# Order of TensorE work in the steps of the two wide cross-attentions: averages first, then transposes, with the turn by features between them

## The chip, the cores and the metric

The kernel runs on one core of a Trainium2 chip. Its time is the device time of one execution in microseconds (us). The core has a matrix engine (TensorE, in the profile PE for its matmuls and PEld for the loads of its stationary operand), a vector engine (VectorE, DVE), a scalar engine (ScalarE, ACT), GpSimd (POOL) and a sync engine (SP) that here only issues DMAs. Matmuls write to PSUM, which has eight banks of 128 x 512 float32; VectorE and ScalarE read it from there. Each engine works through its own list of instructions in order and waits for the others by semaphores.

## The reference

A stack of four layers, each a cross-attention to a context, a mixer and a feed-forward part, works on x of 16 sequences x 64 queries x 256 features. All of it is float32. The change touches the cross-attention of the last two layers, which have the same form (8 heads of 64, context of 16 sequences x 1024 keys x 192 features):

```python
B, Nq, _ = x.shape
q = (x @ Wq).reshape(B, Nq, HEADS, DIM_HEAD)
k = (context @ Wk).reshape(B, context.shape[1], HEADS, DIM_HEAD)
v = (context @ Wv).reshape(B, context.shape[1], HEADS, DIM_HEAD)
sim = jnp.einsum('bihd,bjhd->bhij', q, k) * SCALE
attn = jax.nn.softmax(sim, axis=-1)
out = jnp.einsum('bhij,bjhd->bihd', attn, v)
out = out.reshape(B, Nq, HEADS * DIM_HEAD)
return out @ Wo + bo
```

It is applied as `x = x + attention(_layernorm(x), ctx_768, ...)`. In the layer called L2 a linear recurrence over the 64 queries follows, in L3 a state-space model (Mamba) and then a dense feed-forward.

## The kernel before

`heads64` (lines 420 to 592) computes this attention, once in `L2_xattn_attn` (line 1681) and once in `L3` (line 1840). The keys and values are never formed. The matrix Wk is multiplied into the queries (`queries`, `with_keys`), so that the scores are a product with the raw context, and Wv is multiplied into Wo (`output_matrices`), so that the softmax averages the raw context rows of 192 features.

A tile is 128 rows: two sequences of 64 queries. There are 8 tiles (NT), and each tile has four steps (line 550): a sequence `par` of the two, and a group `g` of four heads. In a step the work on four heads of one sequence is two blocks of 128 rows (2 heads x 64 queries) by 1024 keys. A step's work is spread over three rounds of the loop (line 552). In one round stand

- `now`, the step whose scores are computed: `scores` (line 497) issues 16 matmuls into two PSUM tiles `sc` of two banks each, and `exp_rows` (line 220) then takes each row's maximum on VectorE (`nmx`) and the exponential with its sum on ScalarE (`p`), block 0 first, then block 1;
- `one`, the step of the last round: its two `p` are transposed by `keys_first` (line 228), each in two halves of four 128 x 128 transposes into PSUM tiles `ps_t` (two banks in turn), which are copied out as `pT`: the first half by VectorE and the second by ScalarE, or both by ScalarE where `spare_dve` is set. Then `averages` (line 516) multiplies block 0's `pT` with the context: 8 matmuls of 128 x 192, whose result `o` is divided by the sums into `on`, 192 columns by VectorE (line 522) and 64 of them once more by ScalarE (line 523);
- `two`, the step before that: `averages` of its block 1, and for both blocks `by_features` (line 526), the turn by features: two transposes of `on` into one PSUM tile, copied out in three pieces (`onT`, `onT2`) by `evict` (line 58), which alternates between VectorE and ScalarE, or takes ScalarE alone under `spare_dve`. After a tile's last step `output` multiplies with the output matrices.

`self.misc` hands out the PSUM tile for `averages`, `by_features`, and (in L2) `with_keys`, `queries` and the recurrence. There are two such banks, used strictly in turn, so a new tile waits until the readers of the one before the last are done. In L3 they are called `halves`; there `queries` and `with_keys` take their PSUM (`large`) from the same two banks as `ps_t`.

The order of TensorE's instructions is the order in which the program issues them (`manual_schedule`, line 542). The order on VectorE and ScalarE is set by the scheduler of the framework. `breathe(0)` to `breathe(3)` are places at which another computation puts its next piece: in L2 the recurrence (`go`, line 1801, not at place 3), in L3 the state-space model (`go`, line 2065). The latter first prepares a chunk and then issues items of three VectorE instructions and two exponentials each; while such items are going, `spare_dve` is set. Neither the pieces nor their number per round depend on anything but the count of places passed.

The DMAs of the context are issued by `fetch_cut_ctx` (line 406) ahead of `breathe(0)`, into two buffers in turn.

Of the kernel before, what the change touches and what calls it, by code (L numbers as in the profile page):

```python
# [42 lines left out]
class Net:  # L43
# [376 lines left out]
    def heads64(  # L420
# [12 lines left out]
        def output_matrices():  # L433
            for g in range(2):
                ps = [large([128, 2, D]) for _ in range(2)]
                for v in range(2):
                    hp = 2 * g + v
                    for r in range(2):
                        rows = slice(64 * r, 64 * r + 64)
                        self.mm(ps[r][:, v, :], [(wvT[rows, hp, :128], wo[rows, hp, :])])  # L440
                for r in range(2):
                    to = wvo.rearrange("p (hp r) f -> p r hp f", r=2)[:, r, 2 * g : 2 * g + 2]
                    self.evict(to, ps[r])
            for g in range(2):
                ps = large([128, 2, D])
                for v in range(2):
                    hp = 2 * g + v
                    for r in range(2):
                        rows = slice(64 * r, 64 * r + 64)
                        self.mm(ps[rows, v, :], [(wvT[rows, hp, 128:], wo[rows, hp, :])])  # L450
                self.evict(wvo2[:, 2 * g : 2 * g + 2], ps)

        def normalized(i):

            if i < 2:
                self.carry(i, self.lp.tile([128, 4, D], F32, tag="p", bufs=2, name="p"))
            else:
                self.carry(i, tag="o", bufs=1)
            mv, rs = self.norm_tile(self.xs[:, i, :], 1e-5)
            o = self.lp.tile([128, D], F32, tag="o", bufs=1, name="o")  # L460
            nc.vector.tensor_scalar(o, self.xs[:, i, :], mv[:, 0:1], rs, ALU.subtract, ALU.mult)
            nc.gpsimd.tensor_tensor(self.xs[:, i, :], self.xs[:, i, :], bo, ALU.add)
            hT[i] = self.lp.tile([128, 2, 128], F32, tag="hT", bufs=2, name="hT")
            self.evict(hT[i], self.transposed(o))

        def queries(i):
            ps = large([128, 4, 128])
            for m in range(4):
                self.mm(
                    ps[:, m, :], [(wq[:, c, m * 128 : (m + 1) * 128], hT[i][:, c, :]) for c in range(2)],  # L470
                )
            qT = self.lp.tile([128, 4, 128], F32, tag="qT", bufs=1, name="qT")
            nc.vector.tensor_scalar(qT, ps, 64**-0.5, None, ALU.mult)  # L473

            qpT[i] = qT, [
                [self.lp.tile([128, 8, S], F32, tag=f"qp{n}", bufs=3, name=f"qp{n}") for _ in range(2)]
                for n in range(2)
            ]

        def with_keys(i, n):  # L480

            qT, qp = qpT[i]
            ps = [large([128, 4, 2, S]) for _ in range(2)]
            for hp in range(4):
                for r in range(2):
                    rows = slice(64 * r, 64 * r + 64)
                    self.mm(
                        ps[r][:, hp].rearrange("p b q -> p (b q)"),
                        [(wkT[rows, hp, 128 * n : 128 * n + 128], qT[rows, hp, :])],
                    )  # L490
            for r in range(2):
                for par in range(2):
                    self.evict(
                        qp[n][par].rearrange("p (hp r) q -> p r hp q", r=2)[:, r], ps[r][:, :, par, :]
                    )

        def scores(i, par, g, ctx, between):
            qp = qpT[i][1]
            sc = [self.lps.tile([128, KEYS], F32, tag="sc", bufs=2, name="sc") for _ in range(2)]
            for n in range(2):  # L500
                if n and between is not None:
                    with_keys(*between)
                for u in range(2):
                    h = 4 * g + 2 * u
                    for kh in range(2):
                        rows = slice(64 * kh, 64 * kh + 64) if n else slice(0, 128)
                        at = slice(KEYS, KEYS + 512) if n else bass.ts(kh, 512)
                        nc.tensor.matmul(  # L508
                            sc[u][:, bass.ts(kh, 512)],
                            qp[n][par][rows, h : h + 2, :].rearrange("p h q -> p (h q)"), ctx[0][rows, at],  # L510
                            start=n == 0, stop=n == 1,
                        )
            sums = [self.one_sum() for _ in sc]
            return sums, [self.exp_rows(*x) for x in zip(sc, sums)]

        def averages(pT, sums, ck):
            o = self.misc([128, CD])
            self.mm(o, [(pT[:, t, :], ck[:, t, :]) for t in range(NK)])
            r = self.small.tile([128, 1], F32, name="av_r")
            nc.vector.reciprocal(r, sums)  # L520
            on = self.lp.tile([128, 256], F32, tag="on", bufs=2, name="on")
            nc.vector.tensor_scalar(on[:, :CD], o, r, None, ALU.mult)
            nc.scalar.activation(on[:, CD:], o[:, 128:CD], AF.Copy, scale=r)
            return on

        def by_features(on, onT, par, hp):
            ps = self.transposed(on)
            self.evict(onT[0][:, 2 * hp : 2 * hp + 2, par, :], ps[:, 0, :].rearrange("p (h q) -> p h q", q=S))
            for r in range(2):
                rows = slice(64 * r, 64 * r + 64)  # L530
                self.evict(onT[1][rows, hp, par, :], ps[rows, 1, 64 * r : 64 * r + 64])
# [10 lines left out]
        with self.tc.manual_schedule(engines={mybir.EngineType.PE}):  # L542
            output_matrices()
            first()
            normalized(0)
            queries(0)
            for n in range(2):
                with_keys(0, n)
            normalized(1)
            steps = [(i, par, g) for i in range(NT) for par in range(2) for g in range(2)]  # L550
            one = two = None
            for k in range(len(steps) + 2):
                x = steps[k] if k < len(steps) else None
                now = None
                if x is not None:
                    i, par, g = x
                    if not par and not g:
                        onT = [
                            self.lp.tile([128, 8, 2, S], F32, tag="onT", bufs=1, name="onT"),
                            self.lp.tile([128, 4, 2, S], F32, tag="onT2", bufs=1, name="onT2"),  # L560
                        ]
                    if not g:
                        ctx = self.fetch_cut_ctx(2 * i + par)
                    now = {"x": x, "ctx": ctx, "onT": onT}
                breathe(0)
                if one is not None:
                    one["pT"] = [self.keys_first(one["p"][0])]
                if two is not None:
                    by_features(two["on"], two["onT"], two["x"][1], 2 * two["x"][2])
                    on = averages(two["pT"][1], two["sums"][1], two["ctx"][1])  # L570
                breathe(1)
                if one is not None:
                    one["pT"].append(self.keys_first(one["p"][1]))
                breathe(2)
                if now is not None:
                    between = (i + 1, g) if par and i + 1 < NT else None
                    now["sums"], now["p"] = scores(*x, ctx, between)
                breathe(3)
                if two is not None:
                    by_features(on, two["onT"], two["x"][1], 2 * two["x"][2] + 1)  # L580
                if one is not None:
                    one["on"] = averages(one["pT"][0], one["sums"][0], one["ctx"][1])
                if two is not None and two["x"][1:] == (1, 1):
                    output(two["x"][0], two["onT"])
                    finished(two["x"][0])
                if now is not None and (par, g) == (0, 1):
                    if i + 2 < NT:
                        normalized(i + 2)
                    if i + 1 < NT:
                        queries(i + 1)  # L590
                one, two = now, one
# [1834 lines left out]
```

## Time and profile before

| | us |
|---|---|
| runs shown | 2939.41, 2947.67, 2950.96; median 2947.67 |
| the profiled execution, its own time | 2943.51 |
| its span in the trace | 2941.7 |
| busy: PE, PEld | 2681.1 (91%), 1973.5 |
| busy: DVE, ACT, POOL | 1466.4 (50%), 1043.0 (35%), 306.1 (10%) |
| `heads64` in L2, from its first scores on | 1294 to about 1806 |
| `heads64` in L3, from its first scores on | about 2016 to 2700 |
| mean TensorE clock granted over the span, as a share | 0.952 |

A line of the profile's timeline gives start and duration in us, the engine, the line of the kernel, the operation with its tiles (written <- read), and in brackets the idle time of that engine before it and what ended it. Rows of the same kind that follow each other are merged; such a row's duration reaches from the first start to the last end, and the end of a matmul is modelled, so matmul groups overlap a little. What counts for TensorE is therefore the distance from start to start. A matmul at line 69 is that of the helper `mm`: `ctx,pT` are averages, `w,onT` the output, `hT,w` the queries, `qT,w` the queries with keys. Line 179 with `ident,on` is the turn by features, line 235 a transpose of exponentials, line 508 the scores, line 2054 a sum of the state-space model.

### The profile page before, as it was taken

What the parts mean: (1) busy time and instruction counts of PE and PEld (TensorE: products, weight loads), DVE (VectorE), ACT (ScalarE), POOL (GpSimd) and SP (SyncE); (2) the same over time, 40 slices, a digit from 0 to 9 for tenths busy, and PEclk for the clock granted to TensorE, in tenths of its full rate; (3) what the DMA queues carried; (4) which work ended last, traced back from release to release, by engine and by line L of the source; (5) the groups of instructions that cost most, each with busy time, mean ns of one, the idle gap of its engine ahead of it and who ended that gap; (6) DMA issues with size and microseconds to landing.
All of it is one profiled execution on the core that took longest, in us unless ns stands there. A gap on an engine that the chain in (4) does not pass through costs nothing. (4 is left out here: it accounts for less than half of the span.)

```text
span 2941.7 us, 42834 instructions
## 1 busy us (share of the span) xinstructions
PE 2681.1 (91%) x16972; PEld 1973.5 (67%) x16972; DVE 1466.4 (50%) x3120; ACT 1043.0 (35%) x2350; POOL 306.1 (10%) x407
## 2 busy tenths in 40 slices
PE   7887898999999898989999998898998898888999
PEld 3556785566666586867777776795766666666777
DVE  2555113666666653234444444323446656658593
ACT  1322121555555441223333322122334455455330
POOL 1111232100000011310101001101001000000000
PEclk9897998999999997989999999899999999999999
DMA  8512772111010113811111111552213213121110
GB/s 235 167 49 81 279 270 73 35 30 36 27 37 23 41 37 137 298 53 45 56 56 45 44 54 61 214 218 75 69 43 87 70 42 94 54 73 29 57 45 8
DMA packets 79221, 253.57 MB, mean 86 GB/s; under 512 B 15151, under 2 KB 26954, under 8 KB 69290
## 3 DMA queue, kind: packets, MB, share of 16 engines
q1 hardware_dynamic: 59562, 165.01, 18.1%
q0 software_dynamic: 13312, 80.28, 8.0%
q10 hardware_dynamic: 6144, 5.51, 0.5%
q8 instruction: 135, 2.21, 0.3%
q14 instruction: 68, 0.56, 0.1%
HBM read 233.80 MB, written 14.82 MB: 85 GB/s over the span
## 5 line engine op out<-in xcount | busy, mean ns | idle before, releaser
L223 DVE TENSOR_REDUCE nmx<-sc 128x1 f32<-128x1024 f32 x264 | 311.9, 1219 | 223.8 <-PE sc L508 132.8
L225 ACT ACTIVATE p<-sc,nmx 128x1024 f32<-128x1024 f32 x264 | 294.6, 1116 | 312.8 <-DVE nmx L223 312.2
L508 PE MATMUL sc<-ctxT,qp 128*128 128x512 f32 (+1 forms) x1024 | 357.0, 603 | 0.0
L508 PEld LDWEIGHTS sc<-ctxT,qp 128*128 128x128 f32 (+1 forms) x1024 | 139.5, 190 | 154.8 <-issue 152.6
L69 PE MATMUL halves<-ctx,pT 128*128 128x192 f32 x1024 | 188.0, 339 | 9.4 <-DVE xs L89 4.0
L69 PEld LDWEIGHTS halves<-ctx,pT 128*128 128x128 f32 x1024 | 175.7, 200 | 12.3 <-DVE xs L89 4.5
L69 PE MATMUL misc<-ctx,pT 128*128 128x192 f32 x1024 | 177.6, 327 | 0.5 <-DVE qT L473 0.5
L235 PE MATMUL ps_t<-ident,p 128*128 128x128 f32 x1088 | 147.6, 278 | 25.2 <-ACT p L225 17.6
L69 PEld LDWEIGHTS misc<-ctx,pT 128*128 128x128 f32 x1024 | 166.3, 191 | 2.2 <-DVE qT L473 1.0
L2020 ACT ACTIVATE da<-rep,al 128x252 f32<-128x252 f32 x256 | 115.1, 498 | 117.8 <-DVE x L2030 101.1
L2030 DVE TENSOR_TENSOR_SCAN x<-da,x 128x512 f32<-128x512 f32 x128 | 152.9, 1220 | 3.4 <-ACT da L2020 2.8
L237 ACT COPY pT<-ps_t 128x512 f32<-128x512 f32 x182 | 104.3, 585 | 140.3 <-PE ps_t L235 138.4
L235 PEld LDWEIGHTS ps_t<-ident,p 128*128 128x128 f32 x1088 | 127.4, 143 | 39.2 <-ACT p L225 22.4
L235 PE MATMUL misc<-ident,p 128*128 128x128 f32 x1024 | 138.3, 280 | 13.4 <-ACT p L225 6.3
L235 PEld LDWEIGHTS misc<-ident,p 128*128 128x128 f32 x1024 | 110.7, 141 | 39.7 <-ACT p L225 14.4
L160 POOL TENSOR_TENSOR ln_rs<-ln_ve,nhalf 128x1 f32<-128x1 f32 x80 | 45.7, 576 | 691.7 <-DVE ln_ve L158 552.7
L237 ACT COPY pT<-misc 128x512 f32<-128x512 f32 x128 | 75.0, 586 | 115.4 <-PE misc L235 115.0
L69 PE MATMUL ps_h<-r,w 128*128 128x256 f32 x512 | 113.4, 381 | 0.0
L69 PE MATMUL gu<-dT,wa 128*128 128x128 f32 (+1 forms) x864 | 104.8, 280 | 3.9 <-ACT dT L64 2.4
L239 DVE COPY pT<-misc 128x512 f32<-128x512 f32 x128 | 88.3, 690 | 38.8 <-PE misc L235 28.2
L69 PEld LDWEIGHTS ps_h<-r,w 128*128 128x128 f32 x512 | 96.6, 190 | 15.9 <-issue 2.5
L69 PEld LDWEIGHTS gu<-dT,wa 128*128 128x128 f32 (+1 forms) x864 | 98.3, 185 | 11.2 <-ACT dT L64 4.8
(478 smaller groups left out, 4479.1 us busy)
## 6 DMA issues: line engine op xcount, KB each, us to landing
ctx<-in_ctx SPq DMA_DIRECT2D x48, 768.0 KB
ctxT<-in_ctxT SPq DMA_DIRECT2D x48, 512.0 KB
w<-in_L2f_W SPq DMA_DIRECT2D x24, 1024.0 KB
rep<-dus SPq DMA_DIRECT2D x256, 64.0 KB
ctxT<-in_ctxT SPq DMA_DIRECT2D x16, 768.0 KB
ctxT<-in_ctxT SPq DMA_DIRECT2D x96, 128.0 KB
ys<-yb ACTq DMA_DIRECT2D x40, 128.0 KB
bc_rep<-bcs SPq DMA_DIRECT2D x32, 128.0 KB
```

The costliest lines, as they stand in the source:

```text
L69: self.nc.tensor.matmul(out, lhsT, rhs, start=n == 0, stop=n == len(pairs) - 1)
L160: nc.gpsimd.tensor_tensor(rs, ve, self.nhalf, ALU.pow)
L223: self.nc.vector.tensor_reduce(nmx, sc, AX.X, ALU.max, negate=True)
L225: self.nc.scalar.activation(p, sc, AF.Exp, bias=nmx, accum_out=sums)
L235: self.nc.tensor.transpose(ps[:, u, :], p[:, at : at + 128], self.ident)
L237: self.nc.scalar.copy(pT[:, 4 * g : 4 * g + 4, :], ps)
L239: self.nc.vector.tensor_copy(pT[:, 0:4, :], ps)
L508: nc.tensor.matmul(sc[u][:, bass.ts(kh, 512)], qp[n][par][rows, h : h + 2, :].rearrange("p h q -> p (h q)"), ctx[0][rows, at], start=n == ...
L2020: nc.scalar.activation(da[:, g, :, 1:], now[j][:, 0, :].rearrange("p (b s) -> p b s", s=S)[:, :, 1:], AF.Exp, scale=al[:, col : col + 1],)
L2030: nc.vector.tensor_tensor_scan(flat, da.rearrange("p g b s -> p (g b s)"), flat, 0.0, ALU.mult, ALU.add)
```

## The change

In each round, `averages` of the step before last (block 1) moves from behind the first transposes to the very start, ahead of them. The turn by features of that step's block 0, which stood between those transposes and the averages, now follows behind `breathe(1)`, ahead of the second transposes. So the order of a round's first half goes from

first transposes, turn by features, averages, `breathe(1)`, second transposes

to

averages, first transposes, `breathe(1)`, turn by features, second transposes.

The second half of the round (scores, the turn by features of block 1, averages of the last step's block 0, output, the next tile's queries) stays as it was. No instruction is added or taken away.

```diff
                 breathe(0)
+
+
+                if two is not None:
+                    on = averages(two["pT"][1], two["sums"][1], two["ctx"][1])
                 if one is not None:
                     one["pT"] = [self.keys_first(one["p"][0])]
+                breathe(1)
                 if two is not None:
                     by_features(two["on"], two["onT"], two["x"][1], 2 * two["x"][2])
-                    on = averages(two["pT"][1], two["sums"][1], two["ctx"][1])
-                breathe(1)
                 if one is not None:
                     one["pT"].append(self.keys_first(one["p"][1]))
                 breathe(2)
```

## The prediction

> **What bounds the kernel now.** I read the page's busy times first, then the longest waits of TensorE, then the timeline of single rounds in each of the two stages, and last the table of busy time and granted clock by stretches.
>
> ```profile
> PE 2681.1 (91%) x16972; PEld 1973.5 (67%) x16972; DVE 1466.4 (50%) x3120; ACT 1043.0 (35%) x2350; POOL 306.1 (10%) x407
> ```
>
> TensorE is busy 91% of the span and no work leaves it, so only its waits can move the time. The two attentions differ in these. In L2 (1294 to 1806) the timeline of TensorE shows waits of 0.3 us or more only some two or three times in the 63 us of a tile. An ordinary round there, with VectorE and ScalarE beside it:
>
> ```profile
> 1344.69 2.77 PE L69 MATMUL misc<-ctx,pT 128*128 128x192 f32 x16
> ...
> 1346.12 1.11 ACT L225 ACTIVATE p<-sc,nmx 128x1024 f32<-128x1024 f32 x1
> ...
> 1347.23 0.19 ACT L64 COPY onT<-misc 64x64 f32<-64x64 f32 x1
> 1347.29 1.04 PE L235 MATMUL ps_t<-ident,p 128*128 128x128 f32 x8
> ...
> 1347.55 0.23 DVE L62 COPY onT<-misc 64x64 f32<-64x64 f32 x1
> ...
> 1348.38 0.65 PE L179 MATMUL misc<-ident,on 128*128 128x128 f32 x2
> ```
>
> The first transposes (1347.29) follow the averages (1344.69) after 2.60 without a wait: their exponentials are long done. But the copies of the turn by features that preceded those averages end only at 1347.78, since one stands on ScalarE behind the second exponential, and the last waits for it.
>
> In L3 the state-space model fills VectorE and ScalarE from about 2250 on, and there TensorE waits for the exponential:
>
> ```profile
> 2317.20 2.77 PE L69 MATMUL halves<-ctx,pT 128*128 128x192 f32 x16
> ...
> 2319.07 2.35 DVE L223 TENSOR_REDUCE nmx<-sc 128x1 f32<-128x1024 f32 x2
> 2320.32 1.11 ACT L225 ACTIVATE p<-sc,nmx 128x1024 f32<-128x1024 f32 x1 [1.42 <-DVE nmx L223]
> ...
> 2321.43 0.57 ACT L64 COPY onT<-halves 128x128 f32<-128x128 f32 x3
> ...
> 2321.58 1.09 PE L235 MATMUL ps_t<-ident,p 128*128 128x128 f32 x8 [1.61 <-ACT p L225]
> ...
> 2323.89 0.58 PE L179 MATMUL halves<-ident,on 128*128 128x128 f32 x2 [1.22 <-DVE on L522]
> ```
>
> The maximum (2319.07) comes late because VectorE works off items first; two waits follow, 1.61 and 1.22. There are five such rounds (first transposes at 2279, 2300, 2321, 2488, 2509).
>
> **The change, part by part.** Call X the averages at a round's end, Y those that move to the next round's start. Nothing is added; one order changes. DMAs don't move: they are issued ahead of place 0. Y frees its context buffer 1 to 3 us earlier, which only helps the load that waits for it on SP.
>
> *1. A new wait ahead of Y.* The PSUM bank of Y is that of the turn by features before X. Y could start at 1347.29 and must wait for the copy ending at 1347.78. Where `output` waits for such a copy, it starts 0.05 later (copy to 1374.55, matmul at 1374.60), and averages that waited last 2.87, not 2.77. So 0.49 + 0.05 + 0.10 = 0.64 here. The same subtraction in the 23 such rounds of L2 and the 6 of L3 ahead of the state-space model gives 0.5 to 1.4, mean 0.72: 29 x 0.72 = **+20.9**.
>
> *2. A wait that goes.* The turn by features follows its `on` by one group of transposes today: 1348.38 - 1347.29 = 1.09, where 0.88 is the distance without waiting (2192.99 to 2193.87), and 0.48 on to the next averages, where it is 0.22 (2193.87 to 2194.09). That is 0.47; where the copies fall the other way (1424.55) 0.24. With Y in between it is covered: 29 x -0.36 = **-10.4**. What is late next is part 3.
>
> *3. Transposes closer together.* Both `ps_t` banks are filled by the first transposes, and the second ones need them empty. Today Y (2.6) lies between. Without work at place 1 only the turn does: second transposes 0.88 + 0.22 = 1.10 after the first. The first copy ends 1.33 after its transposes start (1351.46 to 1352.79), with 0.05 for the handover 1.38: 0.28 late, 0.05 more for a start after a wait. ScalarE's copy ends 1.66 after, when 1.82 is needed, so it adds nothing. In 32 rounds (the 29 and three tile ends with place 1 empty): **+10.6**. Bounds: 0 if VectorE's copy gains 0.3, double if `on` of Y, ahead of it on VectorE, is held up. Queued behind these copies are only the maxima of the next scores, which end 5.5 later.
>
> So the regular rounds lose 20.9 - 10.4 + 10.6 = **+21**.
>
> *4. Queries in L3.* They share the banks of `ps_t`; the second half of the first transposes waits for their eviction: 0.35, 0.35, 0.99, 1.96, 2.89, 0.40 = 6.9. Y (2.6) now lies between, 6.6 could go. In the rounds of 1.96 and 2.89 VectorE is working off items, and part returns at its next result: **-5**, between 0 and -6.6.
>
> *5. Place 1.* Pieces there wait for `on` of Y to leave its bank: 0.74, 1.38 in L2, 2.16, 3.27, 1.50, 1.27, 0.68 and four of 0.46 in L3. One group of transposes (0.88) now lies between, so at most -7.7. The longest two belong to chunks being normalized, where VectorE's chain is late anyway; half: **-3.8**.
>
> *6. The five rounds that wait for exponentials.* Y would start behind the three copies (2322.00 plus 0.05) instead of the transposes at 2321.58. Taken alone, the wait grows. But the cycle runs through VectorE, whose list is in order:
>
> ```profile
> 2303.76 5.01 PE L69 MATMUL halves<-ctx,pT 128*128 128x192 f32 x16
> ...
> 2308.88 0.42 DVE L522 TENSOR_SCALAR on<-halves,av_r 128x192 f32<-128x192 f32 x1 [5.79 <-PE halves L69]
> ...
> 2327.19 0.42 DVE L522 TENSOR_SCALAR on<-halves,av_r 128x192 f32<-128x192 f32 x1 [3.44 <-PE halves L69]
> ```
>
> VectorE stands idle until Y is done, and only then takes up items and the next maxima. From one such end to the next it is 2327.61 - 2309.30 = 18.3. Afterwards: items 9.8 (2309.30 to 2319.07), maximum and exponential 2.4 (to 2321.43), copies 0.6, then Y and its `on`, 0.1 + 2.6 + 0.7: 16.2. TensorE's own work in such a round is about 15 (Y 2.6, transposes 1.8, sum 1.9, turns 0.5, scores 5.5, X 2.6). So up to -2.1 a round, -10.5 in five; the rounds at tile ends have more on VectorE: **-8**.
>
> *7. The clock.* The 5.01 above is Y at half clock, after gaps of 2.21 and 0.87:
>
> ```profile
> 2302.00:2306.00 4.00, 3.13 (x11) 2.69 (x10) 0.48 (x2) 2.42 (x8) 0.00 (x0) 0.50 0.00 0
> ```
>
> The last column but two is the granted clock, 0.50. The Trainium skill ("TensorE: Matmul & The Clock Gate", the section on HAM oscillation) speaks for a limit of about 3.4 us of idleness; by it only the gap of 4.41 would cost, and shortening the others brings nothing. By the row, 2.21 was enough and costs 5.01 - 2.77 = 2.2; the same at 2488 (gap 2.21, averages 5.29), but not at 2321 (1.61 and 1.22). The row decides. The danger is that one wait before Y of over 2 us replaces two short ones; with the shorter cycle it comes out near 1. I take one of the two saved, **-2.2**; bounds -4.7 and +2.2 (the round of 2321 falls too).
>
> *8. Turns by features late in L3.* Waits of 0.39, 0.98, 0.99, 1.05, 2.31 (5.7) are covered by Y. Against it, under `spare_dve` both copies of part 3 are ScalarE's, 0.58 each behind `on`: 0.9 in some five rounds with no sum at place 1. **-1.2**.
>
> Late L3: -5 - 3.8 - 8 - 2.2 - 1.2 = **-20**. Together +1. The dense stage after it is bound by TensorE, so what the attentions gain or lose reaches the end. Against the profiled execution's own 2943.5 this gives 2944.5. The median of the runs stands 4.2 above that execution; taking half of it, I predict **2947**.
>
> **Rivals.** *Slower, about 2965.* The wait before Y: late L3 keeps its period, because Y's bank is emptied by copies that stand on ScalarE behind the first exponential, and ScalarE's `pT` copies now stand behind both `on`. Then +21 stands alone: 2943.5 + 21. For it: 2321.43, copies end 0.42 after today's start. Against it: VectorE's idle 5.79 and 3.44 ahead of `on`. It decides over 0.5% (14.7) when late L3 gives back less than about 6, some 1.2 for each of the five rounds.
>
> *Faster, about 2924.* Part 3 is hidden, and late L3 gains all: 21 - 10.6 - (6.6 + 7.7 + 10.5 + 4.7 + 1.2) = -20. For it: gaps of 60 us in all on TensorE from 2250 to 2690. Against it: there one wait follows another (1.61, then 1.22), so that a removed wait is often not gained.
>
> *It does not do what it says:* TensorE's order is written by hand, so Y does stand first; only that Y's bank were another could void part 1, and the banks are used strictly in turn. Then both sides nearly vanish: within 0.5%.
>
> **How the numbers follow.** Within 0.5%, about what a measurement of this kernel tells from no change: 0.48, of which 0.02 the void case; slower 0.31; faster 0.21. The likeliest case alone spans 2932 to 2962. The range reaches to both rivals, 2924 and 2968, and leaves out what lies beyond them.
>
> **What would show it.** Part 1: in L2 the averages that follow averages start about 3.2 after them, not 2.6, with a wait on `onT`. Part 2: turn by features 0.22 long before second transposes. Part 3: second transposes waiting on `pT`. Part 6: rounds of 16 instead of 18 after 2290, and no row of averages of 5 us. I am wrong if L3 from its first scores to the last isn't about 15 shorter or L2 not about 15 longer.

## The result, and the profile after

The kernel after takes 2961.19 us (median of 8 runs, 2954.29 to 2965.85), the kernel before 2942.32 (8 runs, 2939.41 to 2950.96). The ratio is **1.0058**, 95% interval 1.0044 to 1.0072: slower, by about 17 us. The forecast was 2947 and no measurable change; what came is close to the slower rival's number. The prediction's own sign of being wrong came up as well: L2 is 17.6 longer, as it said, but L3 only 2.7 shorter instead of about 15. The profiled execution of the kernel after has a span of 2960.1 and a time of 2961.91, which is 18.4 above the one of before.

The page's busy times:

```profile
PE 2696.5 (91%) x16972; PEld 1979.2 (67%) x16972; DVE 1467.7 (50%) x3120; ACT 1041.6 (35%) x2350; POOL 304.6 (10%) x407
```

TensorE is busy 15.4 longer with the same 16972 instructions. More time that counts as busy, with no work added, is matmuls that ran slower or whose recorded ends lie further from their starts; it has to be looked for by stages. From one round's first scores to another's, in the timelines:

| us | before | after | change |
|---|---|---|---|
| L2, first scores to last | 497.9 | 515.5 | +17.6 |
| L3, first scores to those of step 13 | 220.7 | 222.7 | +2.0 |
| L3, step 13 to last scores (late L3) | 425.3 | 420.6 | -4.7 |
| all else, of the execution's own time | 1799.6 | 1803.0 | +3.4 |

So late L3 gave back little. An ordinary round of L2 of the kernel after, from its timeline:

```profile
1346.68 2.77 PE L69 MATMUL misc<-ctx,pT 128*128 128x192 f32 x16
...
1348.11 1.11 ACT L225 ACTIVATE p<-sc,nmx 128x1024 f32<-128x1024 f32 x1
...
1349.22 0.19 ACT L64 COPY onT<-misc 64x64 f32<-64x64 f32 x1
...
1349.55 0.23 DVE L62 COPY onT<-misc 64x64 f32<-64x64 f32 x1
...
1349.83 2.87 PE L69 MATMUL misc<-ctx,pT 128*128 128x192 f32 x16 [0.38 <-DVE onT L62]
...
1352.53 1.04 PE L235 MATMUL ps_t<-ident,p 128*128 128x128 f32 x8
...
1353.17 0.69 DVE L239 COPY pT<-ps_t 128x512 f32<-128x512 f32 x1
...
1353.40 0.38 PE L179 MATMUL misc<-ident,on 128*128 128x128 f32 x2
...
1353.92 1.09 PE L235 MATMUL ps_t<-ident,p 128*128 128x128 f32 x8
```

Three things can be read off, all by starts. Y (1349.83) follows X (1346.68) by 3.15 where 2.60 is the distance without waiting: the last copy of the turn (1349.55) stands behind ScalarE's copy, and that behind the second exponential. The first transposes follow Y by 2.70, not 2.60. The second transposes (1353.92) follow the first by 1.39, where two groups back to back would need 1.10; the copy that empties their bank (1353.17 + 0.69 = 1353.86) ends just ahead of them. The bracket of Y says 0.38, less than the 0.55 by starts, because the matmuls' ends are modelled.

In late L3 the waits have changed places. The longest of TensorE before, from 2240 to 2710 (total, times, longest), and then of the kernel after in the same stretch:

```profile
PE ps_t L235 <- ACT p L225: 12.3, 5, 4.4
PE halves L69 <- ACT onT L64: 7.5, 4, 2.6
PE halves L179 <- DVE on L522: 7.0, 6, 2.3
PE halves L179 <- ACT on L523: 6.7, 4, 3.3
...
PE ps_t L235 <- DVE qT L473: 5.2, 3, 2.9
```

```profile
PE halves L69 <- ACT onT L64: 20.4, 9, 3.9
PE ps_t L235 <- ACT pT L237: 10.0, 6, 2.7
PE halves L2057 <- ACT on L523: 5.0, 4, 3.5
PE halves L179 <- ACT on L523: 2.9, 3, 2.2
```

The waits for `p` and for `qT` are gone and those for `on` have shrunk in sum; in their place Y waits for copies of the turn, and transposes wait for ScalarE's copies to `pT` (10.0, where the list of before shows none). Busy time and granted clock (the last column but two) of late L3, in the table by stretches, before and after:

```profile
2237.80:2663.10 425.30, 368.74 (x2001) 264.80 (x2000) 272.48 (x431) 215.84 (x522) 21.67 (x33) 0.96 0.24 71
```

```profile
2260.40:2681.00 420.60, 373.85 (x2000) 268.48 (x1999) 271.81 (x434) 214.43 (x522) 20.45 (x33) 0.96 0.24 70
```

TensorE's idle time (stretch less busy) fell from 56.6 to 46.7, by 9.8. Its busy time rose by 5.1 for the same matmuls. One of the five rounds that used to wait for the exponential, after:

```profile
2324.79 0.42 DVE L522 TENSOR_SCALAR on<-halves,av_r 128x192 f32<-128x192 f32 x1 [2.86 <-PE halves L69]
...
2326.08 1.92 PE L2057 MATMUL halves<-x,stack 128*32 128x256 f32 x16 [0.46 <-ACT on L523]
2327.17 1.29 DVE L2029 TENSOR_TENSOR x<-rep,bc_rep 128x512 f32<-128x512 f32 x2 [1.96 <-PE halves L2057]
...
2336.45 2.35 DVE L223 TENSOR_REDUCE nmx<-sc 128x1 f32<-128x1024 f32 x2
2337.70 1.11 ACT L225 ACTIVATE p<-sc,nmx 128x1024 f32<-128x1024 f32 x1 [1.42 <-DVE nmx L223]
...
2338.80 0.57 ACT L64 COPY onT<-halves 128x128 f32<-128x128 f32 x3
...
2339.43 4.19 PE L69 MATMUL halves<-ctx,pT 128*128 128x192 f32 x16 [1.86 <-ACT onT L64]
...
2343.66 0.42 DVE L522 TENSOR_SCALAR on<-halves,av_r 128x192 f32<-128x192 f32 x1 [2.54 <-PE halves L69]
```

Y waits 1.86 for copies that ScalarE does only after the first exponential, and then takes 4.19 instead of 2.87. In the five rounds Y waits 2.87, 2.68, 1.86, 2.68 and 2.31, and lasts 4.55, 4.55, 4.19, 4.55 and 4.48.

Yet these five rounds are not where the busy time rose. In them it is 87.9 before and 88.6 after, since three of them had lost clock before the change too, and more of their matmuls than Y. The stretches at half clock before (after start, end and length, the first number is TensorE's busy time), and one of the five after:

```profile
2277.59:2284.41 6.82, 4.78 (x18) 4.31 (x19) 2.41 (x6) 4.71 (x13) 0.08 (x1) 0.50 0.01 2
2301.48:2308.31 6.83, 5.96 (x22) 5.48 (x21) 0.48 (x2) 2.94 (x8) 0.00 (x0) 0.50 0.00 0
2489.21:2496.04 6.83, 5.65 (x19) 5.49 (x20) 0.48 (x2) 2.36 (x8) 0.00 (x0) 0.50 0.00 0
```

```profile
2340.81:2344.22 3.41, 3.41 (x14) 3.32 (x13) 0.72 (x2) 0.32 (x1) 0.00 (x0) 0.50 0.00 0
```

If a matmul at half clock takes twice its time, half of the busy time in such stretches is lost. As an estimate, that is 8.2 in the five rounds before (of 16.4 busy) and 8.5 after (of 17.1). Over all of late L3 the same sum gives 14.2 before and 17.2 after. The last two rounds lost nothing before and lose 3.9 now; the other rounds change both ways.

### The profile page after: what moved, and what is told of

The parts are those of the page before. It is cut to its first block, busy times and chain, and to the rows that moved or that the text cites. A ratio compares the mean times of both kernels' runs of the same rounds, so it can differ in the third digit from the quotient of the medians.

```text
span 2960.1 us, 42834 instructions
## 1 busy us (share of the span) xinstructions
PE 2696.5 (91%) x16972; PEld 1979.2 (67%) x16972; DVE 1467.7 (50%) x3120; ACT 1041.6 (35%) x2350; POOL 304.6 (10%) x407
## 5 line engine op out<-in xcount | busy, mean ns | idle before, releaser
L223 DVE TENSOR_REDUCE nmx<-sc 128x1 f32<-128x1024 f32 x264 | 311.8, 1219 | 231.5 <-PE sc L508 139.3
L69 PE MATMUL misc<-ctx,pT 128*128 128x192 f32 x1024 | 179.6, 329 | 10.1 <-ACT onT L64 5.9
L69 PEld LDWEIGHTS misc<-ctx,pT 128*128 128x128 f32 x1024 | 164.9, 190 | 18.1 <-ACT onT L64 10.1
L235 PE MATMUL ps_t<-ident,p 128*128 128x128 f32 x1088 | 150.5, 281 | 24.5 <-ACT pT L237 10.2
L2029 DVE TENSOR_TENSOR x<-rep,bc_rep 128x512 f32<-128x512 f32 x128 | 84.6, 688 | 52.7 <-PE halves L2057 42.0
```

The lines of the kernel that those rows point to most:

```text
L69: self.nc.tensor.matmul(out, lhsT, rhs, start=n == 0, stop=n == len(pairs) - 1)
L223: self.nc.vector.tensor_reduce(nmx, sc, AX.X, ALU.max, negate=True)
L235: self.nc.tensor.transpose(ps[:, u, :], p[:, at : at + 128], self.ident)
L2029: nc.vector.tensor_tensor(h, now[j][:, 1:2, :].to_broadcast([128, 2, CHUNK]), bc[:, 0, states, :], ALU.mult)
```

## The experiments

Each ratio is to the kernel before, run on the same chip; "late L3" is read from one profiled execution of each kernel. The short diffs are against the changed kernel; Y is written as `on = averages(...)`.

### The turn alone

Only the turn by features moves; the averages stay behind the first transposes.

```diff
+                first transposes          # one["pT"] = [self.keys_first(one["p"][0])]
                 on = averages(...)
-                first transposes
                 breathe(1)
                 by_features(two["on"], ...)
                 second transposes
```

> The first transposes stay at the round's start, the averages of the step before last follow directly, then place 1, the turn by features, the second transposes: only the turn moves. Theory (the new loss is the wait of the averages for the PSUM bank of the turn before them): the first transposes, 0.88, now cover most of the 0.5 to 0.7 that the copies need beyond, and the turn is covered by the averages. In L2 the averages wait for nothing, a round is 0.24 to 0.47 shorter than before, L2 in all 8 to 10 us; in late L3 the second of the two waits goes as well. Ratio to before about 0.995 (0.992 to 0.998), some 2927 us. Rival (any order that puts second transposes right behind the turn is slower, because of the banks of the transposes): 1.003 or more.

Measured: 2909.19, ratio **0.9891** (0.9873 to 0.9908): faster than both kernels. L2 takes 487.8, late L3 402.9. A round of L2 has no wait left (TensorE's timeline):

```profile
1345.85 2.77 PE L69 MATMUL misc<-ctx,pT 128*128 128x192 f32 x16
1348.45 1.04 PE L235 MATMUL ps_t<-ident,p 128*128 128x128 f32 x8
1349.32 2.77 PE L69 MATMUL misc<-ctx,pT 128*128 128x192 f32 x16
1351.92 0.38 PE L179 MATMUL misc<-ident,on 128*128 128x128 f32 x2
1352.14 1.04 PE L235 MATMUL ps_t<-ident,p 128*128 128x128 f32 x8
```

Each row starts when the one before is through: 2.60, 0.87, 2.60, 0.22. Y covers the copies of `pT`, the first transposes cover the copies of the turn. L2 is 10.1 shorter than before, which is part 2 measured by itself; the gain in late L3, 22.4, was underestimated: the expectation leaves it some 5. Of it, 13.6 is idle time of TensorE, and 7.8 is clock (half of the busy time at half clock: 14.2 before, 6.4 here).

### The copies ahead of Y on VectorE

The order of the change; the three copies of the turn at the round's end are VectorE's, unless `spare_dve` is set.

```diff
+            evict = self.evict
+            if early and not self.spare_dve:
+                evict = nc.vector.tensor_copy
+                self.flip ^= 1
```

> The changed order, but the three copies of the turn that stands behind the scores are VectorE's alone wherever ScalarE is not the one that makes all copies (L2 and early L3), so that none stands behind the second exponential. Theory: the copies end some 0.5 before the averages of the next round could start, their wait goes, a plain round of L2 is 0.6 to 0.7 shorter than in the changed kernel, 14 to 20 us in all. Ratio to before about 1.000 (0.998 to 1.002). Rival (the loss of L2 comes from the second transposes standing too close behind the first): rounds stay as in the changed kernel, ratio 1.006.

Measured: 2933.61, ratio 0.9969 (0.9956 to 0.9981), a little below the expected range. L2 takes 498.3 instead of 515.5. In TensorE's timeline X and Y have become one row of 32 matmuls:

```profile
1340.25 5.37 PE L69 MATMUL misc<-ctx,pT 128*128 128x192 f32 x32
1345.45 1.04 PE L235 MATMUL ps_t<-ident,p 128*128 128x128 f32 x8
1346.33 0.38 PE L179 MATMUL misc<-ident,on 128*128 128x128 f32 x2
1346.84 1.09 PE L235 MATMUL ps_t<-ident,p 128*128 128x128 f32 x8
```

Part 1 is gone, and part 3 still there: 1346.84 - 1345.45 = 1.39. With this run L2's sum can be taken apart: the turn alone against before -10.1 (part 2), this run against the turn alone +10.4 (part 3), the change against this run +17.3 (part 1).

### Place 1 between Y and the first transposes

```diff
                 on = averages(...)
+                breathe(1)
                 first transposes
-                breathe(1)
                 by_features(two["on"], ...)
```

> The changed order, but place 1 (in L3 the sum of the state-space model) directly behind the averages, ahead of the first transposes. Theory: in late L3 VectorE waits 2.0 to 2.3 us after dividing those averages, because its next item needs the place in SBUF that this sum reads, and the sum now comes 0.9 of transposes and a 0.46 wait later than before the change; with the sum first, that idle time falls below 1 us and late rounds get 1 to 2 us shorter, some 8 to 15 us in all; L2 stays. Ratio to before about 1.002 (1.000 to 1.004). Rival (late L3 gained nothing because of the halved clock behind the wait ahead of the averages, or of the exponentials themselves): ratio 1.005 to 1.007.

Measured: 2961.36, ratio 1.0067 (1.0053 to 1.0081): nothing gained, a miss. Late L3 takes 423.6, and two rounds at tile ends (one of them ahead of late L3) grow by 3.5 and 3.9, since the pieces put there wait for `on` of Y. VectorE's waits for the sums, which were to fall, stay at 28.9 (29.7 in the changed kernel): ahead of the transposes, the sum waits 0.86 for `on` of Y. So this run leaves open what a shorter wait would bring. In one of the five rounds the wait did fall, from 1.96 to 1.49; that round takes 17.1, where it takes 17.6 in the two runs below in which Y runs at full clock behind the longer wait.

### The change in L3 alone

```diff
+                if self.halves is None:
+                    (the old order)
+                else:
+                    (the new order)
```

> The changed order in L3 alone, the old one in L2. Theory (L2 loses some 17 us, L3 neither gains nor loses by more than a few): ratio to before about 1.000 (0.998 to 1.003). Rival (the loss is made in L3): 1.005 or more. If L3 had gained what was forecast: 0.995.

Measured: 2942.19, ratio 1.0005 (0.9995 to 1.0015). L2 is back at 498.4, L3 from first to last scores takes 639.6 against 646.0 before. So the slowdown sits in L2; L3's gain of 6.4 in the profile doesn't show in the medians. Late L3 takes 417.9 here and 420.6 in the changed kernel, with the same order in it: the estimated loss of clock is 14.7 here and 17.2 there. In its last two rounds it is 1.4 here and 3.9 there. A difference of some 3 us between two profiles of late L3 thus means little. The stages outside the two attentions vary by several us from one profiled execution to another (from L2's last scores to L3's first 224.8 to 231.5 in all of them, with before the lowest), more than this gain.

### The clock: filling the wait

Fourteen transposes of the identity matrix, into a bank that nobody reads, stand ahead of Y in the five rounds.

```diff
                 breathe(0)
+                if self.halves is not None and k in (15, 16, 17, 24, 25):
+                    fill = self.room_t([128, 4, 128])
+                    for u in range(14):
+                        nc.tensor.transpose(fill[:, u % 4, :], self.ident, self.ident)
```

> The changed order, and in the five rounds of late L3 whose first averages wait 1.9 to 2.9 us for the copies, 14 transposes of the identity (about 1.5 us, their result unused) are issued just ahead of that wait, to keep TensorE busy. Theory (a part of the forecast gain of late L3 went into the halved clock behind that one wait: the averages take 4.2 to 4.55 us there instead of 2.77): these five groups of averages take 2.8, the five rounds get 1.4 to 1.7 shorter each, L3 from its first to its last scores some 7 us shorter than in the changed kernel (643 to about 636). Ratio to before about 1.004. Rival (the clock is no part of it, the time is set by VectorE's list): the averages are short, but the rounds stay.

Measured: 2950.00, ratio **1.0031** (1.0019 to 1.0043), about 8 us less than the change. The same round, from this kernel's timeline:

```profile
2333.85 1.69 PE L569 MATMUL ps_t<-ident 128*128 128x128 f32 x14
...
2335.25 0.57 ACT L64 COPY onT<-halves 128x128 f32<-128x128 f32 x3
...
2335.88 2.87 PE L69 MATMUL halves<-ctx,pT 128*128 128x192 f32 x16 [0.34 <-ACT onT L64]
```

Y still starts 0.63 after the copies' start, as in 2338.80 to 2339.43; the filling doesn't shorten the wait, it only keeps TensorE at work. Y takes 2.87 in all five rounds, and their sum falls from 102.1 to 93.7 (before: 106.4): by 8.4, and 8.5 was the loss estimated from the granted clock. Late L3 as a whole keeps 6.5 of it (420.6 to 414.1).

### More item buffers

```diff
-        self.n_pT = 3
+        self.n_pT = 2
-            return s.x[s.xn % 6]
+            return s.x[s.xn % 8]
-        s.x = rooms(self.sb, "x", 6)
+        s.x = rooms(self.sb, "x", 8)
```

> The changed order, with 8 instead of 6 buffers x for the items of the state-space model, and 2 instead of 3 buffers pT to make the room (the changed order needs no third: block 1's is read before the next is written). Theory (late L3 gains nothing because VectorE, after dividing the averages at a round's start, waits 2 us for the sum at place 1, which frees the x of its next item and now stands behind the first transposes): VectorE's wait for that sum falls from 29.7 us to under 15, late L3 gets 5 to 15 us shorter; L2 stays. Ratio to before about 1.003 (1.001 to 1.005). Rival (the exponentials' chain and the clock set these rounds): 1.0055 to 1.007.

Measured: 2956.64, ratio 1.0060 (1.0047 to 1.0073), late L3 420.1: no gain, the rival's number. But VectorE's wait for the sums falls only from 29.7 to 23.8, and in four of the five rounds it stays at 1.96 to 3.08. The edit did not take away the wait that it was meant to take away, so neither this run nor the one with place 1 ahead of the transposes refutes that late L3 is held up by the later sum.

### The turn behind the second transposes

```diff
                 breathe(1)
-                by_features(two["on"], ...)
                 second transposes
+                by_features(two["on"], ...)
```

> The changed order, but the turn by features behind the second transposes, so that nothing lies between first and second ones where place 1 is empty. Theory (the second transposes' wait for the banks is one of the terms of the loss, 0.33 a round in the changed kernel): they stand 0.22 closer and wait 0.2 to 0.3 longer, the turn itself costs nothing anywhere; a plain round of L2 stays within 0.1 of the changed kernel's, since that wait grows by as much as the turn behind it takes. L2 within 3 us of the changed kernel. Ratio to before 1.005 to 1.008. Rival (the distance of the transposes is what makes the loss): L2 6 us or more longer.

Measured: 2976.43, ratio 1.0117 (1.0102 to 1.0131). L2 grows by 7.5 against the change, not by less than 3; that is the rival's number. But the second transposes do not start later: they stay 1.38 behind the first, where the copies of `pT` put them. The turn's 0.22 comes on top, in 25 of the 31 rounds (0.17 to 0.28 each), and three others grow by 0.5 to 0.8. The turn in the gap was free; the gap is set by the copies.

### The turn ahead of place 1

The order of the turn alone, but with the turn between Y and place 1.

```diff
+                first transposes
                 on = averages(...)
-                first transposes
-                breathe(1)
                 by_features(two["on"], ...)
+                breathe(1)
                 second transposes
```

> First transposes, averages, turn by features, place 1, second transposes: as the run with the turn alone moved behind the averages and place 1, but the turn ahead of place 1. Theory: L2 as there (488 us from first to last scores), since in most rounds place 1 is empty; in L3 the sum at place 1 comes 0.3 later and the turn's on is as ready. Ratio to before about 0.989 to 0.992.

Measured: 2918.72, ratio 0.9928 (0.9913 to 0.9943), slightly above the expected range. L2 is the same as with the turn behind place 1 (488.2), late L3 9 us longer (412.2), of which some 2.6 is clock. The five rounds don't differ (92.1 and 92.3), so the rest lies in other rounds; what holds those up was not followed.

### Both repairs in late L3

The filling, and the old order in L3's last two rounds. There the change shows its other cost; from the timeline of the kernel after:

```profile
2659.07 1.11 PE L235 MATMUL ps_t<-ident,p 128*128 128x128 f32 x4 [2.52 <-ACT pT L237]
...
2659.98 8.05 PE L508 MATMUL sc<-ctxT,qp 128*128 128x512 f32 x16
...
2679.29 1.97 PE L235 MATMUL ps_t<-ident,p 128*128 128x128 f32 x8 [2.74 <-ACT pT L237]
```

The second transposes wait 2.5 and 2.7 for the banks, where Y stood between the two groups before, and the scores behind the first of these waits take 8.05 instead of 5.52. (The granted clock is halved from 2658.25 to 2665.07. Half of the 5.09 that the scores share with this stretch is 2.55, and they take 2.53 longer, so the doubling assumed above holds here.) The last two rounds are 2.3 and 5.0 longer than before.

```diff
+                late = self.halves is not None and k in (30, 31)
+                (the filling)
-                if two is not None:
+                if two is not None and not late:
                     on = averages(...)
                 first transposes
+                if late:
+                    by_features(two["on"], ...)
+                    on = averages(...)
                 breathe(1)
-                if two is not None:
+                if two is not None and not late:
                     by_features(two["on"], ...)
```

> The changed kernel with two repairs in late L3 only: 14 identity transposes ahead of the waiting averages in the five rounds that wait for exponentials (as in the run before), and the old order in the last two rounds of L3 (steps 30 and 31), where block 1's averages again stand between the two groups of transposes. The output is the reference's. Theory (the forecast gain of late L3 was lost to two things alone: the half clock of the moved averages in five rounds, and the second transposes of the last two rounds that wait 2.5 and 2.7 us for ScalarE's copies, with scores at half clock behind them): late L3 from the scores of step 13 to those of step 31 takes about 407 us (414.1 with the filling alone, less 7), the sum about 2943, ratio 1.0005; no wait of second transposes over 2 us in the last two rounds. Rival (these waits belong to ScalarE's work, whatever the order): the time returns at the next wait, late L3 412 or more, ratio 1.003 as with the filling alone.

Measured: 2949.76, ratio 1.0030 (1.0018 to 1.0042), late L3 411.8: a hair under the rival's 412, and the ratio is the rival's, as with the filling alone. The last round did come back to 16.1 (18.8 with the filling alone), but the one ahead of it stayed at 23.3, for Y now waits there:

```profile
2646.15 4.55 PE L69 MATMUL halves<-ctx,pT 128*128 128x192 f32 x16 [2.93 <-DVE xs L89]
```

So of these two waits one belonged to the order; the other only changed its name.

### The turn alone, with more item buffers

The order of the turn alone, with the edit of the item buffers.

> The order of the run in which only the turn by features moves (first transposes, averages, place 1, turn, second transposes), with eight item buffers x instead of six and two pT buffers instead of three. The output is the reference's. Theory (item buffers don't set the time; what is left in late L3 are waits for exponentials and for `on`): within 3 us of that order with six buffers, ratio 0.988 to 0.990. Rival (VectorE's idle time ahead of items sets the round once the averages stand behind the transposes): 5 us or more faster, ratio 0.987 or below.

Measured: 2914.75, ratio 0.9919 (0.9905 to 0.9932): slower than with six buffers by some 8 as the medians' ratios go (the two profiled executions, 2910.21 and 2912.45, don't show it), a miss in size, in the direction away from the rival. Late L3 takes 415.5 instead of 402.9; two of its rounds are 4.0 and 4.5 longer. In the first of these (TensorE's and VectorE's timeline)

```profile
2258.59 0.48 DVE L1338 SCALAR_TENSOR_TENSOR xs<-back,route_g,xs 128x256 f32<-128x256 f32 x1 [3.15 <-DMA back<-ys,route_at]
...
2261.21 3.49 PE L2055 MATMUL halves<-x,stack 128*32 128x256 f32 x16 [3.69 <-ACT onT L64]
```

VectorE has the next tile's rows ahead of `on` in its list, waits 3.15 for their DMA, and TensorE's sum waits 3.69 and then runs at half clock, 3.49 instead of 1.92. Whether more buffers or one `pT` fewer set this order wasn't tried apart.

## Why the prediction was wrong

**Regular rounds: right.** Over 29 rounds the sum was +20.9 - 10.4 + 10.6; for the 23 plain ones of L2 and its three tile ends that is +16.6 - 8.3 + 8.6 = +16.9, and L2 lost 17.6. Taken apart by runs, it is +17.3, -10.1 and +10.4: each part is right in mechanism, and that the sum comes within 0.7 is partly luck, since parts 2 and 3 are both some 1.8 larger than forecast and cancel. *Part 1:* averages behind averages start 3.15 after them, as said. *Part 2:* with the turn alone, plain rounds shrink by 0.24 to 0.51, where 0.24 to 0.47 were worked out. *Part 3:* first to second transposes 1.39 against 1.38. Its size is short: two tile ends lose 1.9 each, since VectorE's list has the normalizations of the next tile and (line 1757) of the recurrence ahead of the copy to `pT`:

```profile
1389.19 0.84 DVE L1757 TENSOR_SCALAR os<-xs,ln_mv,ln_rs 128x256 f32<-128x256 f32 x1
...
1390.28 0.68 DVE L239 COPY pT<-ps_t 128x512 f32<-128x512 f32 x1
...
1391.02 1.09 PE L235 MATMUL ps_t<-ident,p 128*128 128x128 f32 x8 [1.67 <-DVE pT L239]
```

**Late L3: the failed step.** Parts 4 to 8 were to bring -20. L3 from first to last scores changed by -2.7; less its six regular rounds (6 x 0.69 = +4.1), these parts brought about -6.8. By rounds, the five that waited for exponentials were to bring -10.2 (parts 6 and 7) and brought -4.3; the last two rounds grew by 7.3, where part 8, for all of late L3, had -1.2; all other rounds together brought about -9.8, where parts 4 and 5 had -8.8. So the miss of 13 lies in the five rounds and in the last two.

*Parts 4 and 5* (-5, -3.8): the waits for `qT` are gone, those for `on` fell. What the parts named did happen; the two can't be separated in the round lengths.

*Part 6* (-8) **is the first step that failed.** It set the cycle from one division of Y's averages to the next at 16.2: items 9.8, maximum and exponential 2.4, copies 0.6, Y and its `on` 3.4. In the round shown above the cycle takes 18.9: 11.2 (2325.21 to 2336.45), 2.4, 0.6 and 4.7. Two terms are off, and the first is the 9.8. Before, the items of this round started 0.49 behind `on`, since the sum that they wait for stood right behind Y:

```profile
2309.79 1.29 DVE L2026 TENSOR_TENSOR x<-rep,bc_rep 128x512 f32<-128x512 f32 x2 [0.49 <-PE halves L2054]
```

The change puts the first transposes between Y and that sum. The prediction counted this only as a gain, in part 5, and left the 9.8 as it was; now VectorE waits 1.96 for the sum (2327.17), and in three other of the five rounds 3.0 to 3.1 instead of 1.9. With the filling, which keeps Y at full clock, the cycle is still 17.55, and this term of it still 11.2. Over the five rounds, outside of the clock, about -4.6 came instead of -8. That this wait is what holds the cycle is read from the trace; the two runs that were to shorten it hardly did.

*Part 7, the clock* (-2.2), **is the second.** It named the danger, "one wait before Y of over 2 us replaces two short ones", and then took a wait of about 1, from the cycle of 16.2. With the longer cycle the wait is 1.86 to 2.87, and all five rounds lost clock. It also took the loss before from two groups of averages (2.2 and 2.5), and left out the transposes, sums and scores at half clock beside them, and the round with the gap of 4.41. By the granted clock the five rounds lose 8.2 before and 8.5 after: +0.3, not -2.2. The filling shows that the 8.5 are real, as these rounds then get 8.4 shorter. With the last two rounds (3.9; there the trace alone speaks, and with the change in L3 alone the same rounds lost 1.4) and smaller changes both ways, late L3 has +3.0 of clock. The row was rightly preferred to the rule of about 3.4 us of idleness (the Trainium skill, "TensorE: Matmul & The Clock Gate", HAM oscillation): by the rule none of these five waits would have cost anything.

*Part 8* (-1.2) counted 0.9 in five rounds for the second transposes' wait on ScalarE's copies, 4.5; this wait came to 10.0, more than half of it in the last two rounds. Ahead of `on`, and so of these copies, stood VectorE's items, and in the last round a `da` exponential of ScalarE as well. The run with both repairs shows that of its occurrences in these two rounds only one was the order's.

The rest of the miss is +3.4 in stages that the change doesn't touch, where profiles differ among themselves by as much.

**The rival.** "Slower, about 2965" had the number and much of the mechanism. Y's bank is indeed emptied behind the first exponential, `pT` copies do stand behind `on`, and the five rounds gave back 0.9 each, under the 1.2 that it named as its limit. Late L3 didn't quite keep its period: in the two of these rounds that lost no clock before, the kernel with the filling takes 17.6 and 18.0 instead of 18.3 and 19.0. "Faster" failed with part 3, which isn't hidden, and with late L3.

The 2.1 added for the median were of the wrong sign: over eight runs the median of before lies 1.2 below its profiled execution.

## What to carry to other kernels

An order of matmuls is a cover for copies. Before a group moves, ask for both of its neighbours what copy ran under it; here Y covered the copies of `pT`, and the gain of covering the turn's copies was to be had by moving the turn alone (0.9891), while moving Y with it gave that away twice: once ahead of Y (17.3 in L2), once ahead of the second transposes (10.4). Where waits are merged into one, price the slower matmuls behind it along with the wait, and count all matmuls at half clock in the kernel before in the same way. And when a term of a cycle is taken from the old trace (the 9.8 here), ask what released its start, and whether the change moves that.

## What the runs showed of the hardware

Equal waits did not cost the same. Behind the same wait as in the round shown above (1.86, then 4.19), the kernel with more item buffers ran at full speed:

```profile
2334.41 2.87 PE L69 MATMUL halves<-ctx,pT 128*128 128x192 f32 x16 [1.86 <-ACT onT L64]
```

In the run with the turn behind the second transposes, Y took 2.87 after waits of 3.14 and 2.68, but 4.55 after another of 2.68. The granted clock tells the cases apart. In each of the twelve traces, every change of it lies, within 0.01 us, on one grid of 3.41 us, and the grid starts at a different offset from the program in each. In the kernel after, the step ahead of the stretch at half clock shown above (2340.81 to 2344.22):

```profile
2337.40:2340.81 3.41, 1.55 (x10) 1.38 (x9) 1.73 (x5) 2.87 (x7) 0.00 (x0) 1.00 0.00 0
```

With more item buffers, the same wait is cut in two by the grid:

```profile
2329.77:2333.18 3.41, 2.77 (x18) 2.48 (x16) 3.41 (x5) 1.83 (x5) 0.00 (x0) 1.00 0.38 100
2333.18:2336.59 3.41, 2.18 (x13) 2.18 (x14) 1.24 (x4) 2.68 (x8) 0.00 (x0) 1.00 0.00 0
```

TensorE is busy 1.55 of 3.41 (45%) in the step ahead of the halved one, and 81% and 64% where nothing is lost. The wait of 3.14 that cost nothing is cut in the same way, and the wait of 2.68 that cost 1.7 lies in one step, with 21% busy. With the two attentions of all twelve traces cut into the steps of their grid, from first to last scores, all 99 steps at full clock in which TensorE was busy less than 40% were followed by a step at half clock; of those busy 40% to 50%, 15 of 36 were; of those above, none of 3734. This is a count from these stages of this kernel alone; between the two attentions, where other matmuls run, some busier steps were followed by half clock too. A step at half clock in which TensorE has work throughout costs half of 3.41, 1.7 us. The Trainium skill ("TensorE: Matmul & The Clock Gate", the part on the HAM clock gate) describes a window of 3413 ns that runs freely; the traces agree with both.

With 14 identity transposes in the gap, Y took 2.87 in all ten cases of the two runs that had them.
